# Deformable attention, local part: the interpolation factors and the query copies change engines, and the products of the factors change place

## The chip, the cores and the metric

The kernel runs on one core of a Trainium2 chip. A core has five engines that run side by side, each through its own queue in a fixed order: TensorE (PE in the profile; PEld is its weight load), VectorE (DVE), ScalarE (ACT), GpSimd (POOL), and SyncE (SP), which here only issues DMAs. They wait for one another through semaphores. The metric is the device time of one execution in microseconds; the median of three runs of the kernel before is 7593.62 us (7591.17 to 7601.04).

## The reference, cut to what matters

The model has four layers, each a mixer and a feed-forward part, on x of shape (4, 64, 64, 128). The change touches the mixer of layer 0 alone. Queries, keys and values are 1x1 convolutions followed by depthwise 3x3 ones. For each pixel, each of 4 heads of 32 channels looks at 9 points of the key and value images, placed on a 3x3 grid with step d = 1, 3, 5, 7 for the four heads and moved by a learned offset (dy, dx). A point between pixels is read bilinearly, and multiplied by a learned mask:

```
py, px = pixel + d * grid + offset            # per head, 9 points
sample = mask * sum over the 4 corners of (1 - |wy|) (1 - |wx|) image[corner]
logits = <query, sampled key> / sqrt(32);  p = softmax over the 9 points
out    = projection(sum over points of p * sampled value);  x = x + out
```

If no offset is over 1 in size, the corners of all 9 points lie in a small window round the pixel. The kernel finds the greatest offset, and runs a local program if it is at most 1, a general one with gathers if not. With these inputs the local one runs. In it, the weight of the neighbour at distance i = -1, 0, 1 from the grid point is a hat function: max(0, 1 - |offset - i|), for y and x apart, and the bilinear weight is the product of the two.

## The kernel before, in words

The stages run one after another. Function `deformable_near` is the local program; it occupies about 667 to 1723 us of the profiled span. It works on pairs of image rows, 128 pixels, one a partition: 128 steps T (4 images x 32 row pairs), in chunks c of four steps (c = T // 4), and 14 further steps (LAG) in which the second half of the work runs out.

Per step, the first half:
- `products` (L729) copies the queries of the row pair into qm, one of two tiles, spread so that eight columns of pixels at a time meet their own band of keys: two copies per step, on POOL (L737).
- `product` (L754): 64 matmuls on PE (L766) give S, the products of each pixel's query with a band of keys in three rows times four, for the four heads. S has one buffer a head, so the next step's product waits for its copy.
- `copy_products` (L772): four copies on ACT (L776) into band, double buffered by chunk.

Per chunk:
- `offsets` (L686) loads the offsets and masks of four steps (tile of) through SP.
- `hats` (L691) and `rows_of_hats` (L703) make the factors on POOL, L697 to L716: hat for x and y, three values each, and hy, the y factors times mask, widened to four rows, since the 128 pixels of a step are two rows and the lower one (a bit of the partition number, tile row) is shifted by one.
- `hat_products` (L718): four products on POOL (L724), one a head, make H[point, 4 rows, 3 columns], the weights of 12 neighbours. H is double buffered.
- `attention` (L778), on DVE: copies under a predicate (L785) shift each partition's band to its own columns; twelve products with H (L787) and a reduction (L794) give the logits lg, less their maximum (L804).
- `spread` (L807): the exponential on ACT (L810), the normalisation on DVE, then the weights p times H are written into dense rows A, nine products for heads 1 to 3 (L817); head 0, whose points overlap, through t0 (L823) and twelve copies and additions (L827 to L830).
- `write` (L832) sends A to DRAM, `read_dense` (L840) reads it back turned so that each step has its dense matrix D.

Per step, the second half, 14 steps later: `transpose` (L872, twelve on PE, three copies dt on ACT at L880), `weigh` (L884, 96 matmuls or fewer with the value blocks vb, L898), and once a chunk `values_done` (L905, copy oT), `projection` (L916, PE L919, ACT copy L921, two additions on POOL L922 and L923) and `store`.

The order is set by the loop at L947: `step(T, first, do, every)` calls a part at T = first, first + every and so on. `block` chains the PE blocks of a step, and `behind` and `tc.issue_after` tell the scheduler that a part isn't to be issued before a given instruction. Beyond that the scheduler of the language orders each engine's queue, so that the queues, and not the source alone, say what stands behind what. In ACT's queue of the steady part the exponential of chunk c - 1 stands between the band copies of the first and of the second step of chunk c.

Of the kernel before, what the change touches and what calls it, by code (L numbers as in the profile page):

```python
# [608 lines left out]
def deformable_near(k, dr, x, y, qd, kd, vd, od, masks, w_proj, b_proj):  # L609
# [25 lines left out]
    with ExitStack() as ctx:  # L635
# [14 lines left out]
        for t in qms:  # L650
            nc.gpsimd.memset(t, 0.0)
        row = wp.tile([128, 1], F32, tag="row", name="row")
        nc.vector.tensor_copy(row, bit[:, 0, 0, 3:4])

        As = []
        for i in range(2):
            As.append([wp.tile([128, 4, WB[g], 4, 3], F32, tag=f"A{i}{g}", name=f"A{i}{g}") for g in range(4)])
            for t in As[i]:
                nc.vector.memset(t, 0.0)

        dd = [[dr.tile([128, 4 * PP[g] + 12], F32, tag=f"dd{i}{g}", name=f"dd{i}{g}") for g in range(4)] for i in range(3)]
# [10 lines left out]

        Hs, bands, outs, vblocks, logits, ofs, hat_of, hy_of, queries = {}, {}, {}, {}, {}, {}, {}, {}, {}
        accs, lefts, inputs, project, stores = {}, {}, {}, [], []
# [15 lines left out]

        def hats(c):  # L691

            of = ofs[c]
            hat = hat_of[c] = sm.tile([128, 8, 3, 4, 3, 3], F32, tag="hat", name="hat", bufs=1)
            src = window(of, 0, [[81, 4], [9, 8], [3, 3], [1, 3]])
            part = lambda i: window(hat, i, [[9, 4], [108, 8], [36, 3], [3, 3]])
            nc.gpsimd.tensor_scalar(part(0), src, -1.0, 0.0, op0=ALU.mult, op1=ALU.max)  # L697
            nc.gpsimd.tensor_scalar(part(2), src, 0.0, None, op0=ALU.max)
            flat = hat.rearrange("p s a t n i -> p (s a t n) i")
            nc.gpsimd.tensor_tensor(flat[:, :, 1], flat[:, :, 0], flat[:, :, 2], op=ALU.add)  # L700
            nc.gpsimd.tensor_scalar(flat[:, :, 1], flat[:, :, 1], -1.0, 1.0, op0=ALU.mult, op1=ALU.add)

        def rows_of_hats(c):  # L703

            of, hat = ofs.pop(c), hat_of[c]
            mk = sm.tile([128, 2, 36], F32, tag="mk", name="mk")
            at = lambda i: window(mk, 36 * i, [[0, 4], [1, 36], [0, 3]])
            nc.gpsimd.tensor_copy(mk[:, 0].rearrange("p (a t n) -> p a t n", a=3, t=4), window(of, 72, [[3, 3], [81, 4], [1, 3]]))
            nc.gpsimd.tensor_scalar(mk[:, 1], mk[:, 0], row, None, op0=ALU.mult)
            nc.gpsimd.tensor_tensor(mk[:, 0], mk[:, 0], mk[:, 1], op=ALU.subtract)  # L710
            hy = hat[:, 0:4].rearrange("p s a t n i -> p s (a t n) i")
            h4 = hy_of[c] = sm.tile([128, 4, 36, 4], F32, tag="hy", name="hy", bufs=1)
            nc.gpsimd.tensor_tensor(h4[:, :, :, 0:3], hy, at(0), op=ALU.mult)
            nc.gpsimd.tensor_tensor(hy, hy, at(1), op=ALU.mult)
            nc.gpsimd.tensor_tensor(h4[:, :, :, 1:3], h4[:, :, :, 1:3], hy[:, :, :, 0:2], op=ALU.add)
            nc.gpsimd.tensor_copy(h4[:, :, :, 3], hy[:, :, :, 2])  # L716

        def hat_products(c, groups):  # L718

            if 0 in groups:  # L720
                Hs[c] = sm.tile([128, 4, 36, 12], F32, tag="H", name="H")
            H, hat, h4 = Hs[c], hat_of[c], hy_of[c]
            for g in groups:
                nc.gpsimd.tensor_tensor(  # L724
                    H[:, g].rearrange("p n (a c) -> p n a c", a=4), window(h4, 144 * g, [[4, 36], [1, 4], [0, 3]]),
                    window(hat, 108 * (4 + g), [[3, 36], [0, 4], [1, 3]]), op=ALU.mult,
                )

        def products(T):  # L729
            i = T % 32  # L730
            c, t = divmod(T, 4)
            if t == 0:
                bands[c] = [sm.tile([128, 3, 4, 4, CW[g]], F32, tag=f"band{g}", name=f"band{g}") for g in range(4)]
            qm = qms[T % 2]
            q = queries[T // 4]
            for h in range(2):
                after[0] = nc.gpsimd.tensor_copy(  # L737
                    window(qm, 256 * h, [[32, 2], [72, 4], [1, 8]]),
                    q[:, 2 * (i % 4) : 2 * (i % 4) + 2, 32 * h : 32 * h + 32].rearrange("p y (m x) -> p y m x", m=4),
                )  # L740
# [31 lines left out]
        def copy_products(T):  # L772
            c, t = divmod(T, 4)
            acc = accs.pop(T)
            for g in range(4):
                nc.scalar.copy(bands[c][g][:, :, t], acc[g].rearrange("p (a s) c -> p a s c", a=3))  # L776

# [29 lines left out]
        def spread(c):  # L807
# [13 lines left out]

            t0 = sm.tile([128, 36, 12], F32, tag="t0", name="t0", bufs=1)
            nc.vector.tensor_tensor(t0, H[:, 0], window(lg, 0, [[1, 36], [0, 12]]), op=ALU.mult)  # L823
            for ty in range(3):
                a0 = lambda m0, n: window(A[0], 12 * m0 + ty, [[60, 4], [12, n], [3, 4]])
                tap = lambda tx, s0, n: window(t0, 144 * ty + 12 * tx + s0, [[36, 4], [1, n], [3, 4]])
                nc.vector.tensor_copy(a0(0, 3), tap(0, 0, 3))  # L827
                nc.vector.tensor_copy(a0(3, 2), tap(2, 1, 2))
                nc.vector.tensor_tensor(a0(1, 3), a0(1, 3), tap(1, 0, 3), op=ALU.add)
                nc.vector.tensor_tensor(a0(2, 1), a0(2, 1), tap(2, 0, 1), op=ALU.add)  # L830

# [112 lines left out]
        products(0)  # L944
        hats(0)
        rows_of_hats(0)
        for T in range(128 + LAG):  # L947
            now[0] = T
            with behind():
                step(T, -1, products)  # L950
                step(T, -5, offsets, 4)
                with tc.issue_after(after[0].ins):
                    step(T, 0, lambda c: hat_products(c, (0, 1)), 4)
                    step(T, 1, lambda c: hat_products(c, (2, 3)), 4)
                    step(T, -2, hats, 4)
                    step(T, -1, rows_of_hats, 4)
                step(T, 4, attention, 4)
# [1664 lines left out]
```

## Time and profile before

| what | us |
|---|---|
| median of three runs | 7593.62 |
| profiled execution, time | 7610.45 |
| its span | 7608.4 |
| PE busy | 6501.1 (85%) |
| DVE busy | 4893.8 (64%) |
| ACT busy | 2698.1 (35%) |
| POOL busy | 1932.7 (25%) |
| granted PE clock, mean | 0.895 |

The busy shares are averages over stages with different limits; the stage of the change takes about a seventh of the span. In a row of groups stand the line, engine, operation, tiles, sizes (partitions x elements) and count, then busy time in us and mean ns of one, then the engine's idle time just before and what ended it. A row of the timeline has start and duration in us, engine, line, operation, and in brackets the idle time before it with its releaser; instructions that follow closely are merged (x6 is six).

### The profile page before, as it was taken

What the parts mean: (1) busy time and instruction counts of PE and PEld (TensorE: products, weight loads), DVE (VectorE), ACT (ScalarE), POOL (GpSimd) and SP (SyncE); (2) the same over time, 40 slices, a digit from 0 to 9 for tenths busy, and PEclk for the clock granted to TensorE, in tenths of its full rate; (3) what the DMA queues carried; (4) which work ended last, traced back from release to release, by engine and by line L of the source; (5) the groups of instructions that cost most, each with busy time, mean ns of one, the idle gap of its engine ahead of it and who ended that gap; (6) DMA issues with size and microseconds to landing.
All of it is one profiled execution on the core that took longest, in us unless ns stands there. A gap on an engine that the chain in (4) does not pass through costs nothing. (4 is left out here: it accounts for less than half of the span.)

```text
span 7608.4 us, 157410 instructions
## 1 busy us (share of the span) xinstructions
PE 6501.1 (85%) x63791; PEld 3520.3 (46%) x63791; DVE 4893.8 (64%) x11051; ACT 2698.1 (35%) x6141; POOL 1932.7 (25%) x1794
## 2 busy tenths in 40 slices
PE   7996777875788789899989999798897997998989
PEld 3343666662455543355555555445225234242244
DVE  2213888865377546678855656674884876857877
ACT  3331333333154325411155665565004022041056
POOL 0003666640011100055522222253012112120135
PEclk9997888897789899999988889797997997988989
DMA  4436677772400031310000000001101111111101
GB/s 119 102 84 196 197 233 233 232 223 80 147 1 2 19 68 23 96 39 24 18 15 9 9 10 5 9 1 35 39 20 53 25 40 34 26 33 40 24 23 31
DMA packets 673787, 498.13 MB, mean 65 GB/s; under 512 B 296822, under 2 KB 588600, under 8 KB 669208
## 3 DMA queue, kind: packets, MB, share of 16 engines
q1 hardware_dynamic: 510158, 399.80, 18.8%
q10 hardware_dynamic: 162890, 88.11, 4.4%
q8 instruction: 509, 8.34, 0.5%
q14 instruction: 230, 1.88, 0.1%
HBM read 335.28 MB, written 152.33 MB: 64 GB/s over the span
## 5 line engine op out<-in xcount | busy, mean ns | idle before, releaser
L2491 DVE TENSOR_TENSOR t<-S,q 128x1536 f32<-128x1536 f32 (+3 forms) x608 | 1156.9, 1948 | 122.7 <-PE S L2479 117.5
L2479 PE MATMUL S<-R,L 32*128 32x512 f32 x4096 | 734.8, 651 | 90.0 <-DMA R<-wd 78.5
L2507 PE MATMUL acc<-t,sum 128*32 128x512 f32 x4096 | 639.6, 608 | 0.0
L766 PE MATMUL S<-kpad,qm 32*64 32x288 f32 (+3 forms) x8192 | 379.4, 408 | 191.1 <-ACT band L776 125.5
L2193 PE MATMUL pe<-ew,yT 128*128 128x512 f32 x1024 | 482.2, 606 | 26.2 <-DVE xs L2199 23.1
L785 DVE COPY_PREDICATED band<-bit,band 128x384 f32<-128x384 int32 (+11 forms) x384 | 382.6, 1102 | 175.6 <-ACT band L776 141.7
L1792 PE MATMUL acc<-w,attT 128*64 128x264 f32 x4096 | 485.4, 390 | 10.5 <-DMA xtl<-xtd 10.5
L2479 PEld LDWEIGHTS S<-R,L 32*128 32x128 f32 x4096 | 200.5, 186 | 611.1 <-issue 280.0
L2513 ACT COPY agg<-acc 128x512 f32<-128x512 f32 x32 | 18.8, 586 | 1196.7 <-DMA L<-pd 609.0
L1785 POOL TENSOR_TENSOR w<-xtl,ei 128x528 f32<-128x528 f32 x256 | 332.3, 1320 | 307.6 <-ACT ei L1784 202.9
L2199 DVE SCALAR_TENSOR_TENSOR xs<-pe,gate,xs 128x128 f32<-128x128 f32 x1024 | 332.5, 345 | 97.5 <-PE pe L2193 80.8
L766 PEld LDWEIGHTS S<-kpad,qm 32*64 32x64 f32 x8192 | 278.6, 151 | 245.4 <-issue 141.7
L1788 DVE TENSOR_TENSOR w<-xtl,pe 128x1056 f32<-128x1056 f32 x256 | 320.3, 1251 | 99.2 <-ACT ei L1784 89.0
L1792 PEld LDWEIGHTS acc<-w,attT 128*64 128x64 f32 x4096 | 283.6, 137 | 196.7 <-DVE w L1789 38.6
L2202 ACT ACTIVATE sc<-pe,gate 128x128 f32<-128x128 f32 x1024 | 291.3, 374 | 201.4 <-PE pe L2193 193.3
L2522 POOL TENSOR_TENSOR o<-o,bf 128x512 f32<-128x512 f32 x32 | 40.7, 1271 | 1231.1 <-ACT o L2521 1231.1
L514 PE MATMUL dw<-pad,diag 32*32 32x512 f32 x6912 | 308.4, 613 | 12.2 <-issue 6.1
L2507 PEld LDWEIGHTS acc<-t,sum 128*32 128x32 f32 x4096 | 92.8, 108 | 458.6 <-issue 436.2
L2193 PEld LDWEIGHTS pe<-ew,yT 128*128 128x128 f32 x1024 | 186.2, 194 | 233.5 <-issue 151.1
L880 ACT COPY dt<-pt 128x512 f32<-128x512 f32 x384 | 204.5, 604 | 165.6 <-PE pt L878 165.2
L878 PE MATMUL pt<-ident,D 128*128 128x128 f32 x1536 | 231.6, 304 | 17.5 <-DMA D<-dd 9.2
L1680 PE MATMUL acc<-y,xsp 128*64 128x512 f32 (+1 forms) x1088 | 237.1, 597 | 1.9 <-DVE xsp L1655 1.9
(525 smaller groups left out, 13001.1 us busy)
## 6 DMA issues: line engine op xcount, KB each, us to landing
vb<-vd SPq DMA_DIRECT2D x272, 256.0 KB
D<-dd SPq DMA_DIRECT2D x128, 192.0 KB
D<-dd SPq DMA_DIRECT2D x128, 168.0 KB
D<-dd SPq DMA_DIRECT2D x128, 144.0 KB
w<-in_e_weight_dram ACTq DMA_DIRECT2D x16, 1024.0 KB
w<-in_e_weight_dram SPq DMA_DIRECT2D x16, 1024.0 KB
wd<-s SPq DMA_DIRECT2D x32, 512.0 KB
D<-dd SPq DMA_DIRECT2D x128, 120.0 KB
```

Of the source, the lines that this page charges most:

```text
L514: nc.tensor.matmul(acc[g][32 * c : 32 * c + 32], diag[r, j, tap, :], pads[j][r, y0 : y0 + 8, tx : tx + 64], start=(tap == 0), stop=(tap == 8),
L766: ins = nc.tensor.matmul(acc[g][64 * h : 64 * h + 64].rearrange("p (a s) c -> p a s c", a=3), qm[rows, h, m, :], keys, start=(m == 0), sto ...
L785: nc.vector.copy_predicated(flat[:, :, 0:n], bit[:, 0, :, i : i + 1].to_broadcast([128, 48, n]), flat[:, :, s : s + n])
L1785: nc.gpsimd.tensor_tensor(w2[:, 2:4], xt[:, 2:4, 0:2], window(ei, 0, [[0, 2], [0, 2], [1, 132]]), op=ALU.mult)
L1788: nc.vector.tensor_tensor(w1, xt[:, :, 1:3], window(pe, 0, [[0, 4], [0, 2], [1, 132]]), op=ALU.mult)
L1792: nc.tensor.matmul(acc[b // 2][64 * (b % 2) : 64 * (b % 2) + 64], attT[:, b // 2, hp, 64 * (b % 2) : 64 * (b % 2) + 64], src[:, b].rearran ...
L2193: nc.tensor.matmul(pe[h].rearrange("p e c -> p (e c)"), yT[:, 128 * t : 128 * t + 128], ew[:, 4 * h : 4 * h + 4, :].rearrange("p e c -> p ...
L2199: nc.vector.scalar_tensor_tensor(xt, pe[0][:, e, :], gate[:, t, e : e + 1], xt, op0=ALU.mult, op1=ALU.add)
L2202: nc.scalar.activation(sc[:, e, j, :], pe[1][:, e, :], AF.Copy, scale=gate[:, t, 4 + e : 5 + e])
L2479: nc.tensor.matmul(S[:, j, :], Ls[n % 2][r, ag, :], Rs[n % 2][r, ag].rearrange("p x y -> p (x y)"), start=True, stop=True)
L2491: nc.vector.tensor_tensor(t[:, j0:j1].rearrange("p u (x y) -> p u x y", x=8), S[:, j0:j1].rearrange("p u (x y) -> p u x y", x=8), qf[:, q0 ...
L2507: nc.tensor.matmul(acc[0][32 * h : 32 * h + 32, :], sum4, t[:, j, :], start=(u < 4), stop=(u >= 60))
```

## The change

Five things change, all in `deformable_near`:
1. The factors are made by ACT: for each distance i, Abs of (offset + a constant per partition, tile dist), then once Relu(1 - that). `hats_of_rows` makes the four row factors hy (four Abs, one Relu) at step 4c, `hats_of_columns` the three column factors (three Abs, one Relu) and a copy of the mask at step 4c + 1, both not before the last band copy of that step. The row bit now enters through dist, so the mask is applied once, by one POOL product (`masked`).
2. That product and the first two H products are called at step 4c + 2, the other two at 4c + 3, instead of at 4c and 4c + 1.
3. The query copies into qm go from POOL to ACT.
4. Head 0 is spread through a zeroed tile, shared, in which each point has its own slot: three products, and one reduction that adds up the slots of the same column, in place of t0 and twelve small operations.
5. The projection's result is written over oT instead of into a tile of its own.

The queues that the scheduler makes of it: PE's is the same as before, instruction for instruction. In the steady part POOL's has, per chunk, the masking product, four H products and the two additions of the projection. In ACT's, the first half of a query copy stands ahead of each step's band copies and the second half after them; the row factors stand between the band copies of the first step and the three dt copies ahead of the exponential; the column factors follow the band copies of the second step.

```diff
-        row = wp.tile([128, 1], F32, tag="row", name="row")
-        nc.vector.tensor_copy(row, bit[:, 0, 0, 3:4])
+        dist = wp.tile([128, 7], F32, tag="dist", name="dist")
+        for i in range(4):
+            nc.vector.tensor_copy(dist[:, i : i + 1], bit[:, 0, 0, 3:4])
+            nc.vector.tensor_scalar(dist[:, i : i + 1], dist[:, i : i + 1], 1.0 - i, None, op0=ALU.add)
+        for i in range(3):
+            nc.vector.memset(dist[:, 4 + i : 5 + i], 1.0 - i)
...
+        shared = wp.tile([128, 720], F32, tag="shared", name="shared")
+        nc.vector.memset(shared, 0.0)
...
-        def hats(c):
...
-        def rows_of_hats(c):
...
+        def hats(of, off, t, n, at):
+            for i in range(n):
+                nc.scalar.activation(
+                    window(t, i, [[3 * n, 4], [36 * n, 4], [12 * n, 3], [n, 3]]), window(of, off, [[81, 4], [9, 4], [3, 3], [1, 3]]),
+                    AF.Abs, bias=dist[:, at + i : at + i + 1],
+                )
+            return nc.scalar.activation(t, t, AF.Relu, bias=1.0, scale=-1.0)
+
+        def hats_of_rows(c):
+            hy = sm.tile([128, 4, 36, 4], F32, tag="hy", name="hy", bufs=1)
+            hats(ofs[c], 0, hy, 4, 0)
+            hat_of[c] = [hy]
+
+        def hats_of_columns(c):
+            of = ofs.pop(c)
+            hx = sm.tile([128, 4, 36, 3], F32, tag="hat", name="hat", bufs=1)
+            mk = sm.tile([128, 36], F32, tag="mk", name="mk")
+            with tc.issue_after(hats(of, 36, hx, 3, 4).ins):
+                nc.scalar.copy(mk.rearrange("p (a t n) -> p a t n", a=3, t=4), window(of, 72, [[3, 3], [81, 4], [1, 3]]))
+            hat_of[c] += [hx, mk]
+
+        def masked(c):
+            hx, mk = hat_of[c][1:]
+            nc.gpsimd.tensor_tensor(hx, hx, window(mk, 0, [[0, 4], [1, 36], [0, 3]]), op=ALU.mult)
...
-                after[0] = nc.gpsimd.tensor_copy(
+                nc.scalar.copy(
...
-                nc.scalar.copy(bands[c][g][:, :, t], acc[g].rearrange("p (a s) c -> p a s c", a=3))
+                after[0] = nc.scalar.copy(bands[c][g][:, :, t], acc[g].rearrange("p (a s) c -> p a s c", a=3))
...
-            t0 = sm.tile([128, 36, 12], F32, tag="t0", name="t0", bufs=1)
-            nc.vector.tensor_tensor(t0, H[:, 0], window(lg, 0, [[1, 36], [0, 12]]), op=ALU.mult)
-            for ty in range(3):
...
+            for tx in range(3):
+                nc.vector.tensor_tensor(
+                    window(shared, 13 * tx, [[60, 12], [3, 4], [12, 3]]), window(H, 12 * tx, [[36, 12], [3, 4], [1, 3]]),
+                    window(lg, tx, [[3, 12], [0, 4], [0, 3]]), op=ALU.mult,
+                )
+            nc.vector.tensor_reduce(
+                window(A[0], 0, [[1, 3], [60, 4], [3, 20]]), window(shared, 0, [[240, 3], [60, 4], [3, 20], [1, 3]]), axis=AX.X, op=ALU.add
+            )
...
-            o = sm.tile([128, 4, 128], F32, tag="o", name="o", bufs=1)
+            o = oT
...
-        hats(0)
-        rows_of_hats(0)
...
-                with tc.issue_after(after[0].ins):
-                    step(T, 0, lambda c: hat_products(c, (0, 1)), 4)
-                    step(T, 1, lambda c: hat_products(c, (2, 3)), 4)
-                    step(T, -2, hats, 4)
-                    step(T, -1, rows_of_hats, 4)
+                step(T, 2, masked, 4)
+                step(T, 2, lambda c: hat_products(c, (0, 1)), 4)
+                step(T, 3, lambda c: hat_products(c, (2, 3)), 4)
...
                 step(T, 0, copy_products)
+                with tc.issue_after(after[0].ins):
+                    step(T, 0, hats_of_rows, 4)
+                    step(T, 1, hats_of_columns, 4)
```

More of the change, by code (lines that the diff above doesn't have):

```diff
@@ L671, in deformable_near @@
                 eng.dma_start(dd[i][g][:, 4 * PP[g] : 4 * PP[g] + 12], zero[:, 0:12])
-        Hs, bands, outs, vblocks, logits, ofs, hat_of, hy_of, queries = {}, {}, {}, {}, {}, {}, {}, {}, {}
+        Hs, bands, outs, vblocks, logits, ofs, hat_of, queries = {}, {}, {}, {}, {}, {}, {}, {}
         accs, lefts, inputs, project, stores = {}, {}, {}, [], []
@@ L689, in offsets @@
             nc.sync.dma_start(ofs[c], od[b][:, 4 * c8 : 4 * c8 + 4, :])
-        def hats(c):
[L693 to L701, printed above, removed]
@@ L703, in rows_of_hats @@
-        def rows_of_hats(c):
[L705 to L716, printed above, removed]
+        def hats(of, off, t, n, at):
[5 more added lines that the diff above has]
+            return nc.scalar.activation(t, t, AF.Relu, bias=1.0, scale=-1.0)
@@ L721, in hat_products @@
                 Hs[c] = sm.tile([128, 4, 36, 12], F32, tag="H", name="H")
-            H, hat, h4 = Hs[c], hat_of[c], hy_of[c]
+            H = Hs[c]
+            hy, hx, _ = hat_of[c]
             for g in groups:
                 nc.gpsimd.tensor_tensor(
-                    H[:, g].rearrange("p n (a c) -> p n a c", a=4), window(h4, 144 * g, [[4, 36], [1, 4], [0, 3]]),
-                    window(hat, 108 * (4 + g), [[3, 36], [0, 4], [1, 3]]), op=ALU.mult,
+                    H[:, g].rearrange("p n (a c) -> p n a c", a=4), window(hy, 144 * g, [[4, 36], [1, 4], [0, 3]]),
+                    window(hx, 108 * g, [[3, 36], [0, 4], [1, 3]]), op=ALU.mult,
                 )
@@ L820, in spread @@
                     )
-            t0 = sm.tile([128, 36, 12], F32, tag="t0", name="t0", bufs=1)
-            nc.vector.tensor_tensor(t0, H[:, 0], window(lg, 0, [[1, 36], [0, 12]]), op=ALU.mult)
-            for ty in range(3):
[L825 to L830, printed above, removed]
+            for tx in range(3):
[6 more added lines that the diff above has]
+            )
         def write(c):
```

## The prediction, made before the changed kernel had run

> **What bounds the kernel now.** The stages run one after another: in the timeline no load of the next stage (L50) is issued before 1723.36 us, after the last store of this one. So what this stage gains, the end gains, though the chain of waits is followed back only to 5186 us and never reaches it. I began with the busy time by stretches, for the steady part of the stage, chunks 4 to 30:
>
> ```profile
> core 0: us, PE busy (x) PEld busy (x) DVE busy (x) ACT busy (x) POOL busy (x), PEclk, DMA share, GB/s
> 838.00:1636.00 798.00, 631.23 (x17880) 526.44 (x17880) 650.77 (x1379) 307.11 (x809) 520.72 (x646) 0.88 0.78 231
> ```
>
> DVE is busy 82%, PE 79%, DMA 78%: no engine is full, so something goes round in a ring. The waits (who waited for whom: total us, times, longest) for 860 to 1600 us, 24 chunks:
>
> ```profile
> POOL qm L737 <- PE S L766: 239.9, 65, 7.9
> ACT lg L810 <- DVE lg L804: 205.5, 24, 11.9
> ACT band L776 <- PE S L766: 128.0, 72, 4.8
> DVE band L785 <- ACT band L776: 117.6, 24, 7.6
> ...
> PE S L766 <- ACT band L776: 66.0, 16, 7.1
> ```
>
> 24 times DVE waits for ACT's band copies and 24 times ACT waits for DVE's logits: once per chunk each. The timeline of one chunk shows the ring:
>
> ```profile
> 1125.65 6.11 DVE L785 COPY_PREDICATED band<-bit,band 128x384 f32<-128x384 int32 x6 [5.03 <-ACT band L776]
> ...
> 1144.67 0.31 DVE L804 TENSOR_TENSOR lg<-lg,me 128x144 f32<-128x144 f32 x1
> ...
> 1145.01 0.32 ACT L810 ACTIVATE lg<-lg 128x144 f32<-128x144 f32 x1 [6.56 <-DVE lg L804]
> 1145.24 1.04 ACT L776 COPY band<-S 128x144 f32<-128x144 f32 x4
> ...
> 1145.64 4.48 PE L766 MATMUL S<-kpad,qm 32*64 32x144 f32 x64 [2.40 <-POOL hat L700]
> ...
> 1150.18 1.07 ACT L776 COPY band<-S 128x144 f32<-128x144 f32 x4 [1.95 <-PE S L766]
> ...
> 1151.08 0.18 DVE L830 TENSOR_TENSOR A<-A,t 128x16 f32<-128x16 f32 x1
> ...
> 1154.18 2.20 PE L766 MATMUL S<-kpad,qm 32*64 32x144 f32 x64
> ...
> 1156.43 1.07 ACT L776 COPY band<-S 128x144 f32<-128x144 f32 x4 [1.43 <-PE S L766]
> 1156.74 1.93 DVE L785 COPY_PREDICATED band<-bit,band 128x384 f32<-128x384 int32 x2 [5.48 <-ACT band L776]
> ```
>
> Attention (DVE) takes 1125.65 to 1144.98. The exponential behind it stands in ACT's queue ahead of the band copies of the chunk's second step, so it holds them, and with them the one set of S banks and PE. Then three band copies and two key products (4.48 us at the low clock, 2.20 at the full one) pass before the next attention at 1156.74. (The "POOL hat" behind 1145.64 is one of several semaphores; the copy at 1145.24 is what freed S.) Spreading ended at 1151.3 and DVE then idled 5.48 us. I call attention A and the rest B. Over chunks 4 to 28, read off the timeline in this way, A averages 19.04 us, B 11.58, the period 30.6; 30.68 from exponential to exponential.
>
> Why A is 19: POOL works beside it. DVE's groups by shape, 860 to 1600 us:
>
> ```profile
> L787 DVE TENSOR_TENSOR prod<-band,H 128x144 f32<-128x144 f32 x290 | 105.8, 435 | 0.0
> L785 DVE COPY_PREDICATED band<-bit,band 128x384 f32<-128x384 int32 x24 | 28.7, 1195 | 117.6 <-ACT band L776 117.6
> ```
>
> The same for the last chunk alone (1648 to 1667 us), where POOL has no factor left to make:
>
> ```profile
> L787 DVE TENSOR_TENSOR prod<-band,H 128x144 f32<-128x144 f32 x12 | 2.9, 330 | 0.0
> L785 DVE COPY_PREDICATED band<-bit,band 128x384 f32<-128x384 int32 x1 | 0.6, 605 | 7.0 <-ACT band L776 7.0
> ```
>
> In that chunk A is 15.10 us (1648.52 to 1663.61), with one POOL instruction of 0.79 us beside it.
>
> **What the Trainium skill says.** SBUF — State Buffer, Who interferes with whom: a DVE instruction with two SBUF inputs contends with a GpSimd instruction that reads SBUF, through a lock held for a whole instruction; ACT and PE wait on nobody. The rows above agree (435 against 330 ns, 1195 against 605). TensorE: Matmul & The Clock Gate, What's actually happening: an idle PE falls to half clock; agrees with 4.48 against 2.20 us for the same 64 matmuls. ScalarE: Activation LUTs, Table sets: abs and relu are in every set, so the new calls should load no table; no run here shows it.
>
> **The change, part by part.** Per chunk, POOL loses the factors (mean ns of L697 to L716: 1570+1247+763+611+257+428+269+982+981+880+498 = 8.5 us) and eight query copies (8 x 0.69 = 5.5), 14.0 of 21.3 us (busy 520.72 over 26, 20.0, as some overlap); it gains one masking product as L714 (0.98). What stays is 0.98 + four H products (1.17 each) + the two projection adds (2.6) = 8.3 us.
>
> Where that falls counts. In the changed order PE's sequence is the same instruction for instruction. POOL's is: mask product, four H products, two adds. The mask product waits for ACT's mask copy, which stands behind the exponential: one query half, the band copies, three Abs, oT, a Relu. That is 0.32+0.24+1.07+1.0+0.62+0.55+0.22 = 4.0 us after the exponential starts. H is then ready at 4.0+1.0+4.3 = 9.3 us and the adds end at 11.9, while the next attention starts near 11.5 and reads H 3.6 us later. So POOL moves out of A into B, where DVE only spreads (6.7 us) and idles. A goes from 19.04 to about 15.2.
>
> ACT gains per chunk seven Abs, two Relu, a mask copy and eight query halves. Their price: ScalarE: Activation LUTs, What ACT_TABLE_LOAD costs, gives 280 ns + 0.833 ns an element with a pointer bias, 186 without, 93 less back to back: Abs (144) 0.31, Relu (576, 432) 0.67 and 0.55, mask 0.22, query half 0.24 or less. The exponential of 144 without pointer should cost 306 and takes 323 in the trace. Sum 7x0.31+0.67+0.55+0.22+8x0.2 = 5.2 us, beside 11.8 us busy now (307.11 over 26 chunks): 17 us, under any period here. Bounds for one Abs: 0.23 (the exponential's 323 less 93) and 0.52, an estimate from VectorE's price for elements that stand apart (Vector Engine (DVE) Microarchitecture Reference, Measured stream behaviour on trn2: up to 2.5 against 1.05 ns a column). I take 0.31.
>
> On the ring: a query half (0.24) stands ahead of the band copies twice. Three Abs, Relu, mask and another half stand ahead of the three dt copies, which then end 5.9 us after the exponential instead of 3.5; PE wants them after its product and the projection, at about 5.4 us: 0.3 on average. The four row Abs and their Relu (1.9 us) fall under a PE stretch of 4.9 us before their dt copies are needed: nothing, or 1 us if Abs costs 0.52.
>
> DVE's spreading loses the product t0 and twelve small operations (2.4 us, 1148.86 to 1151.26) for three products (0.28 each, as the nine of L817 in 2.50 us) and a reduction over 720 (0.9, from L794's 1953 ns for 1728): 0.7 less, in the 5 us where DVE idles, so nothing; without that idle time it would be 0.7 a chunk. The lock with POOL may stretch spreading by at most POOL's 5.3 us, to 12. DMAs are the same; the load of the offsets (tile of) moves ahead of two value blocks in SP's queue and now waits for ACT's mask copy, which is done before the spreading that SP awaits just ahead of it. The constants cost under 1 us at the start, behind the wait for the zeroing DMAs (band at 695.29).
>
> **What is late next: PE.** With A at 15.2, ACT could release the key product at 15.2+0.65+0.24 = 16.1 us after attention's start. PE itself, in the 25 chunks from 5 to 29, ends what stands before that product at 12.7 to 19.5 us, mean 16.2. The later of the two, chunk by chunk, averages 16.9; now it starts at 19.7. It then starts with little idle time before it: in the seven chunks where PE idled under 2 us it took 3.8 instead of 4.26 on average; half of those stalls go too, I take 3.3. The rest: 4.0 (projection, weights, transposes, as now) + 0.3 (dt) + 2.33 (second product) + 0.31 + 0.24 (band, query half). Period 16.9+3.3+4.0+0.3+2.33+0.55 = 27.4, against 30.68.
>
> **The sum.** 26 periods from exponential 4 to 30: 26 x 3.3 = 86. The first four (27.4 us each now) lose part of A, but there the H products still fall into A: 2 to 2.5 each, with the first attention (21.3 us, waiting for H) about 12. The last one 2 (its A is 15.1 already). Together 100 us; tail after the last chunk unchanged. The profiled execution took 7610.45 us (span 7608.4), so 7510; taken off the median of the runs, 7593.6, 7494.
>
> **The rivals.** (1) Part of the gain stays out: PE's instruction fetch ("issue" before the key products and the value products, 22.4+37.3 us in 24 chunks) slows as DMA goes from 0.78 to 0.88 of its time, or Abs costs 0.52 and delays dt. PE ready at 17.7 on average and 0.6 more in B: period about 29.2, 26 x 1.5 + 9 = 48 saved: 7546. For it: DMA is the fullest resource after DVE. Against: 263 GB/s occurs in slices now.
> (2) More: the stalls before PE's 16.2 are themselves partly low clock. Period 26.2: 26 x 4.5 + 14 = 131: 7463. PE's busy 24.3 us a chunk is the floor.
> (3) Slower: POOL's five products (5.3 us) and spreading's two-input operations lock each other out in B, and H comes late. Attention reads H 15.1 us after the exponential against 9.3 when ready, so nothing happens until H is 5.8 late, and the gain of 3.3 is gone at 9.1. If each of spreading's 15 products waits for a whole POOL product, H ends near 19: period 31.7, 26 x 1 = 26 lost: 7620. Against: spreading has too few POOL instructions beside it to be held so often.
> (4) It does nothing: A stays at 19 because something else slows DVE. The last chunk speaks against it.
>
> **How the numbers follow.** A difference under 0.2% (15 us) is about what a measurement of this kernel cannot tell from none. Chances: computed case 0.59 (7475 to 7525), rival 1 0.21, rival 2 0.07, rival 3 0.09, rival 4 0.04. Faster 0.87, same 0.04, slower 0.09. The range, 7462 to 7562, leaves out rivals 3 and 4 and the ends of 1 and 2.
>
> **What would show it.** Right: attention near 15.2 us, products near 0.33 us, POOL under 9 us a chunk, period 27 to 28, PE's waits for ACT's band shrunk and "issue" first among PE's waits. Wrong: attention over 17 us; DVE waiting for POOL's H; Abs over 0.5 us; PE waiting for dt by more than 1 us a chunk; a table load beside Abs.

## The result, and the profile after

The changed kernel takes 7537.68 us (median of five runs, 7520.84 to 7547.03), the kernel before 7591.17 on the same chip (7572.84 to 7601.04): a ratio of 0.9931, 95% interval 0.9911 to 0.9951, or 53 us. The forecast was 7494, 44 us less than measured. The measured time lies outside the band of the computed case (7475 to 7525), inside the whole range (7462 to 7562), and close to the 7546 of rival 1.

The profiled executions, 7610.45 and 7520.84 us, are 89 us apart, more than the medians. The reason is outside the stage: the first load of the next stage (L50) is issued at 1723.36 us before and 1670.01 after, 53.3 us earlier, and the other 36 us arise in later stages whose code is the same. So the stage gains about what the medians differ by. Its 53.3 us split like this (A is attention, B what lies between one attention and the next, both over chunks 4 to 28; the exponentials are the ACT rows of L817, L810 before):

| us | before | after | forecast |
|---|---|---|---|
| A | 19.04 | 15.17 | 15.2 |
| B | 11.58 | 13.86 | 12.2 (27.4 less 15.2) |
| period, exponential 4 to 31 | 30.70 | 29.03 | 27.4 |
| gained up to exponential 4 | | 14.9 | 12 |
| gained in the 27 periods | | 45.2 | 88 |
| gained from the last exponential to L50 | | -6.8 | 0 |

Almost all of the shortfall is in B. The busy times by stretches for the steady part of after, 29 instead of 30.7 us a chunk:

```profile
core 0: us, PE busy (x) PEld busy (x) DVE busy (x) ACT busy (x) POOL busy (x), PEclk, DMA share, GB/s
830.00:1570.00 740.00, 615.42 (x17536) 502.05 (x17534) 581.08 (x1118) 416.32 (x1250) 187.18 (x179) 0.90 0.82 245
```

POOL's share is down from 65% to 25%, ACT's up from 38% to 56%. DMA is at 0.82, from 0.78, since the same bytes pass in less time.

The groups of DVE by shape in 24 chunks, 860 to 1560 us (busy time, mean ns of one, idle time before it):

```profile
L794 DVE TENSOR_TENSOR prod<-band,H 128x144 f32<-128x144 f32 x288 | 69.6, 327 | 0.0
L830 DVE TENSOR_TENSOR shared<-H,lg 128x144 f32<-128x144 f32 x72 | 68.2, 1057 | 0.0
...
L792 DVE COPY_PREDICATED band<-bit,band 128x384 f32<-128x384 int32 x24 | 15.6, 650 | 133.6 <-ACT band L783 133.6
```

The products of attention take 327 ns, as they did only in the last chunk before (330), and the first predicated copy 650 instead of 1195. Attention runs free of POOL. But L830, three products of spreading of the same size, take 1057 ns each. The timeline of an undisturbed chunk shows what they meet:

```profile
1052.03 0.32 ACT L817 ACTIVATE lg<-lg 128x144 f32<-128x144 f32 x1 [4.50 <-DVE lg L811]
...
1053.56 3.26 DVE L824 TENSOR_TENSOR A<-H,lg 128x144 f32<-128x144 f32 x9
...
1055.55 0.99 POOL L722 TENSOR_TENSOR hat<-hat,mk 128x432 f32<-128x432 f32 x1 [21.06 <-ACT mk L717]
...
1056.62 3.85 POOL L731 TENSOR_TENSOR H<-hy,hat 128x432 f32<-128x432 f32 x4
1056.66 3.12 DVE L830 TENSOR_TENSOR shared<-H,lg 128x144 f32<-128x144 f32 x3
```

Three DVE products in 3.12 us beside POOL products of 0.98 us: each DVE product lasts as long as one POOL product. The lock (DVE and POOL holding each other up while both work) has moved from attention to spreading, which ends 8.4 us after attention and not 6.7. H is ready at 1060.47, 8.4 us after the exponential.

Where B grew is in the waits, again 24 chunks, 860 to 1560 us (who waited for whom: total, times, longest):

```profile
DVE band L792 <- ACT band L783: 133.6, 24, 15.3
...
PE pt L884 <- DMA D<-dd: 38.4, 53, 3.1
PE out L904 <- issue: 36.0, 27, 3.3
...
PE S L773 <- issue: 15.4, 15, 2.4
...
PE out L904 <- DMA vb<-vd: 6.0, 9, 2.0
...
PE S L773 <- ACT band L783: 3.2, 4, 2.1
```

PE hardly waits for ACT's band copies any more (3.2 us, before 66.0): it no longer stands behind attention. In their place is a wait that the kernel before hardly had: for the loads of D, and some for the value blocks, 44.4 us or 1.85 a chunk. 24 chunks of before, 860 to 1600 us, show D alone:

```profile
PE pt L878 <- DMA D<-dd: 3.7, 2, 3.4
```

The waits for "issue" did not grow.

B is not the same in every chunk: in half of the 25 it is 10.5 to 13 us, in the other half 13 to 21. The timeline of chunk 11, one of the longest (B is 19.8):

```profile
1017.13 0.32 ACT L817 ACTIVATE lg<-lg 128x144 f32<-128x144 f32 x1 [2.34 <-DVE lg L811]
...
1020.16 0.48 PE L884 MATMUL pt<-ident,D 128*128 128x128 f32 x1 [0.68 <-DMA D<-dd]
...
1021.20 2.19 PE L884 MATMUL pt<-ident,D 128*128 128x128 f32 x9 [0.56 <-DMA D<-dd]
...
1023.18 0.54 SPq L759 DMA_DIRECT2D q<-qd  x1
...
1030.10 0.24 ACT L744 COPY qm<-q 128x64 f32<-128x64 f32 x1 [6.09 <-DMA q<-qd]
...
1036.85 3.53 DVE L792 COPY_PREDICATED band<-bit,band 128x384 f32<-128x384 int32 x6 [11.08 <-ACT band L783]
```

PE takes the D loads one at a time as they land. SP had sent these four only just before:

```profile
1013.79 2.63 SPq L850 DMA_DIRECT2D D<-dd  x4
```

This holds in general. For each step I took the time from the end of its last D issue to its first transpose: over 860 to 1560 us the median is 15.9 us in before and 7.3 in after, and at most 6.0 in the 22 steps where PE waits for D. The buffer of D is not what holds the load back: in after it had been free for 16.8 us (median) when the load was issued, in before for 9.8. D is late because it is issued late.

Then ACT waits 6.09 us for a query load that SP issued only at 1023.18, and the band copies stand behind that copy in ACT's queue. Chunks 19 and 27 show the same (6.6 and 6.9 us; the profile puts the first down to a transpose on PE, but it goes away in e5 with the late query load): every eighth chunk (an image has eight), where SP has 38 or 39 DMAs to issue instead of 32 on average. With the query copies on POOL, as before, such a wait would stand in POOL's queue and not ahead of the band copies; no run puts the copies back alone.

### The profile page after: what moved, and what is told of

The parts are those of the page before. It is cut to its first block, busy times and chain, and to the rows that moved or that the text cites. A ratio compares the mean times of both kernels' runs of the same rounds, so it can differ in the third digit from the quotient of the medians.

```text
span 7519.0 us, 156903 instructions
## 1 busy us (share of the span) xinstructions
PE 6475.0 (86%) x63791; PEld 3490.8 (46%) x63791; DVE 4812.9 (64%) x10774; ACT 2842.8 (38%) x6717; POOL 1518.8 (20%) x1218
## 3 DMA queue, kind: packets, MB, share of 16 engines
q14 instruction: 226, 1.85, 0.1%
## 5 line engine op out<-in xcount | busy, mean ns | idle before, releaser
L2518 ACT COPY agg<-acc 128x512 f32<-128x512 f32 x32 | 18.8, 586 | 1192.6 <-DMA L<-pd 855.4
L792 DVE COPY_PREDICATED band<-bit,band 128x384 f32<-128x384 int32 (+11 forms) x384 | 312.5, 929 | 186.4 <-ACT band L783 149.8
L773 PE MATMUL S<-kpad,qm 32*64 32x192 f32 (+3 forms) x8192 | 365.8, 405 | 72.4 <-ACT band L783 37.7
L884 PE MATMUL pt<-ident,D 128*128 128x128 f32 x1536 | 259.8, 319 | 66.3 <-DMA D<-dd 48.4
L884 PEld LDWEIGHTS pt<-ident,D 128*128 128x128 f32 x1536 | 214.6, 203 | 87.6 <-DMA D<-dd 52.3
```

What stands on the lines that cost most here:

```text
L773: ins = nc.tensor.matmul(acc[g][64 * h : 64 * h + 64].rearrange("p (a s) c -> p a s c", a=3), qm[rows, h, m, :], keys, start=(m == 0), sto ...
L792: nc.vector.copy_predicated(flat[:, :, 0:n], bit[:, 0, :, i : i + 1].to_broadcast([128, 48, n]), flat[:, :, s : s + n])
L884: ins = nc.tensor.transpose(pt[:, g, :], D[:, g, ty : ty + 382 : 3], k.ident)
```

## Experiments

The theory after the first look at the trace: attention is shortened by what was forecast, and the loss is in SP's queue, which issues some 33 DMAs a chunk and is occupied 86% of the time (77% before, summed from the durations and the short pauses of its instructions, 840 to 1540 us). The rivals: the DMA engines themselves (bytes), or ACT and PE.

**e1: is it the place of the H products?** Only that is put back.

```
-                step(T, 2, masked, 4)
-                step(T, 2, lambda c: hat_products(c, (0, 1)), 4)
-                step(T, 3, lambda c: hat_products(c, (2, 3)), 4)
+                step(T, 0, masked, 4)
+                step(T, 0, lambda c: hat_products(c, (0, 1)), 4)
+                step(T, 1, lambda c: hat_products(c, (2, 3)), 4)
...
-                    step(T, 0, hats_of_rows, 4)
-                    step(T, 1, hats_of_columns, 4)
+                    step(T, -2, hats_of_rows, 4)
+                    step(T, -1, hats_of_columns, 4)
```

> After, with the mask product and the four H products put back beside attention (their old steps 4c and 4c + 1), the factors two steps earlier; nothing left out. Theory (POOL and DVE hold each other up while both work): attention rises from 15.2 us by the 5 us of POOL work that comes back, by 1.3 to 2.6, to about 17; spreading, which loses it, falls from 8.4 to about 6.7 us. If the time between attentions is set by SP's queue, as I now think, the period stays near 29 and the time within 20 us of 7538; if attention still sets the period, it grows by 1.7 us x 27, to about 7585. Rival (the factors and query copies alone slowed attention, H products do not): attention stays at 15.2, spreading at 8.4.

Measured: 0.999 (0.9978 to 1.0002). All of the gain is gone, with the factors and query copies still on ACT. A is 18.79 us, B 11.99, spreading 5.8. The groups of e1, DVE by shape, 860 to 1600 us:

```profile
L794 DVE TENSOR_TENSOR prod<-band,H 128x144 f32<-128x144 f32 x289 | 141.5, 561 | 0.0
...
L830 DVE TENSOR_TENSOR shared<-H,lg 128x144 f32<-128x144 f32 x72 | 22.8, 438 | 0.0
```

and POOL:

```profile
L731 POOL TENSOR_TENSOR H<-hy,hat 128x432 f32<-128x432 f32 x97 | 101.9, 1079 | 2.0
```

The slow products have changed sides: attention's take 561 ns, spreading's 438. Five POOL products, 1.02 + 4 x 1.08 = 5.3 us, lengthen attention by 3.6: dearer than the 1.3 to 2.6 expected. B falls by 1.9 with it, and the period grows by 1.8 us, to 30.86; that is the 45 us. So the lock is shown, and that attention sets the period when it is long: with 18.8 us of it the rest of the change gains nothing that can be measured. With the longer period PE also waits for the band copies again and hardly for D (860 to 1560 us), and the D loads are issued 18.1 us ahead (median), not 7.3:

```profile
PE S L773 <- ACT band L783: 86.5, 23, 7.3
...
PE pt L884 <- DMA D<-dd: 3.9, 2, 2.3
```

So the new work on ACT doesn't make D late by itself; D is late when as many DMAs and bytes have to pass in a shorter period.

**e2: fewer bytes, as many DMAs.** The value tiles are zeroed once at the start (that edit isn't printed), so what isn't loaded is zero.

```
-                    t[:, q].rearrange("p s c -> p (s c)"),
-                    bass.AP(..., [[10752, 32], [128, 4], [1, 512]]),
+                    t[:, q].rearrange("p s c -> p (s c)")[:, 0:256],
+                    bass.AP(..., [[10752, 32], [128, 4], [1, 256]]),
```

> After, with each load of a value block cut to half of its columns (256 of 512 elements a partition), as many DMAs as before; the other half of the values is left at zero, so that much of the computation is left out. Theory (SP's issuing is what runs late: 33 DMAs a chunk, 24.5 us of a period of 29): hardly any change, period 28 to 29, 7520 to 7540. Rival (the DMA engines are full, 7.0 MB a chunk at 245 GB/s): 15% fewer bytes bring the stretch between attentions from 13.9 to about 10.7, the period to 26.2, the time to about 7463.

Measured: 0.9836 (0.9814 to 0.9858), 72 us less than after. A 15.20, B 12.09, period 27.26. The waits, 860 to 1560 us:

```profile
PE S L776 <- ACT band L786: 26.1, 14, 3.7
...
PE pt L887 <- DMA D<-dd: 9.0, 13, 1.1
```

PE waits for the band copies again, hardly for D. SP's queue is occupied for 90% of this shorter period, so the 86% of after was not a limit in itself. This spoke against the theory of SP's issuing alone.

**e3: as many bytes, more DMAs.**

```
-                nc.sync.dma_start(t[:, q]..., bass.AP(..., [[10752, 32], [128, 4], [1, 512]]))
+                for h in range(2):
+                    nc.sync.dma_start(t[64 * h : 64 * h + 64, q]..., bass.AP(..., [[10752, 16], [128, 4], [1, 512]]))
```

> After, with each load of a value block issued as two DMAs of 64 partitions, same bytes and same packets. Theory (SP's issuing): 8.5 more issues a chunk at 0.6 us are 5 us; SP's 24.5 us become 29.6, the period 31 to 33, the time 7590 to 7650. Rival (DMA engines full, or ACT's new work): no change, 7525 to 7550.

Measured: 1.0096 (1.0069 to 1.0123), 125 us more than after. A is 15.13 still, B 18.62, the period 34.1: 5.1 us longer, for 8.3 more issues a chunk of 0.6 us (0.59 the median of such an issue). The waits of 860 to 1560 us:

```profile
DVE band L792 <- ACT band L783: 220.7, 21, 26.1
...
PE pt L885 <- DMA D<-dd: 129.1, 113, 6.6
```

PE's wait for D is 129 us. This spoke for issuing and against bytes alone, with the DMA engines less busy than in after (0.73, 209 GB/s). Together: bytes and number of DMAs both matter, and D is where either shows.

**e4, e5: the query loads.** e4 issues them from ACT's queue; e5 leaves them with SP, in the same place of its queue, but a chunk ahead.

```
-            nc.sync.dma_start(queries[n], ...)
+            nc.scalar.dma_start(queries[n], ...)
```

> After, with the query loads issued from ACT's queue instead of SP's; nothing left out. Theory (SP's queue late): the three chunks in which ACT waited 6.1 to 6.9 us for a query load, with the band copies behind it, lose that wait, some 8 us each, and SP has one issue of 0.6 us less per chunk: 25 to 40 us faster than after, 7498 to 7513. Rival (the long stretches come from PE and ACT themselves, the query load happens to end beside them): ACT gains 0.6 us of issuing per chunk, 7538 to 7555.

Measured: 0.9974 (0.9962 to 0.9986): 33 us slower than after. A miss, whose reason stands in e4's timeline:

```profile
1143.05 2.99 SPq L841 DMA_DIRECT2D dd<-A  x4
...
1148.70 0.33 ACTq L759 DMA_DIRECT2D q<-qd  x1
...
1149.12 0.24 ACT L744 COPY qm<-q 128x64 f32<-128x64 f32 x1 [9.81 <-DMA dd<-A]
```

By the profile ACT stood there until a write of dd had landed, which has nothing to do with queries. In the trace the DMAs of this stage, of either queue, carry eight completion semaphores in turn, and the DMA that last used the semaphore of a query load is a write of dd in all 24 chunks from 860 us on. I read the wait as the load waiting for that semaphore to come free. With the band copies behind it, ACT lost 71.8 us in 13 such places between 860 and 1560 us. The Trainium skill (DMA: Bandwidth & Descriptors, Issuing engines are not separate DMA queues) says that DMAs from any queue run on the same engines, so that another queue saves the issuing time alone; here it brought less than that, a loss.

```
-            queries[n] = sm.tile([128, 8, 64], F32, tag="q", name="q")
+            queries[n] = sm.tile([128, 8, 64], F32, tag="q", name="q", bufs=3)
...
         rows_of_queries(0)
+        rows_of_queries(1)
...
-                if T % 4 == 1 and T < 124:
-                    rows_of_queries(T // 4 + 1)
+                if T % 4 == 1 and T < 120:
+                    rows_of_queries(T // 4 + 2)
```

> After, with a third query buffer, each query load one chunk earlier in the same place of SP's queue; as many DMAs, nothing left out. In e4 the load on ACT's queue stood waiting there for an unrelated write of dd that had been issued eight DMAs before it, with ACT's band copies behind it, so that run didn't test the query wait. Theory (late query loads cost the three long stretches of B, and hold nothing else): ACT's waits for q of 6.1 to 6.9 us vanish, three stretches are 5 to 8 us shorter: 15 to 24 us faster than after, ratio to before about 0.990 to 0.991. Rival (SP or the DMAs behind it are the bound on average, so that a stall taken away here comes back in the next chunk): within 8 us of after, 0.992 to 0.994.

Measured: 0.9928 (0.9901 to 0.9956): after's time. ACT waits for no query load any more, and B in chunks 11, 19 and 27 falls from 19.8, 21.0 and 19.6 to 15.8, 17.3 and 15.2. But in the chunks behind them it rises from 10.5, 11.2 and 11.0 to 13.6, 14.3 and 14.0: of 12.0 us, 9.2 come back at once. B averages 13.97 us against 13.86. The striking 6 us waits were a symptom.

**e6, e7, e9, e10: a wait in SP's queue.** In after SP waits for the store of x before it can issue the next load of xg, with D loads behind (before had this wait too, 35.3 us). SP's own waits, 860 to 1560 us:

```profile
SPq L876 <- DMA x<-xg: 45.2, 21, 2.8
```

e6 gives xg a third buffer, e7 also calls the query load two steps earlier.

```
-                inputs[0] = sm.tile([128, 4, 128], F32, tag="xg", name="xg")
+                inputs[0] = sm.tile([128, 4, 128], F32, tag="xg", name="xg", bufs=3)
```

> After, with a third buffer for xg, so that its load no longer stands in SP's queue waiting for the store ahead of it to land (46.8 us of SP's time in 24 chunks, 1.9 us a chunk), with D loads behind it. Nothing left out. Theory (SP's queue is late by as much as it is given: 5.0 us of issues more made the period 5.1 longer in e3): the period falls from 29.0 by 1 to 1.9 us, 27 to 50 us faster than after, ratio 0.987 to 0.990. Rival (bytes in flight are the bound, as half the value bytes gave 1.8 us a chunk in e2): SP runs ahead by 1.9 us and then waits for the DMAs that it awaits elsewhere; within 10 us of after, 0.992 to 0.995.

> After, with the third xg buffer and the query load called two steps earlier, which puts it ahead of four D loads in SP's queue, 2.6 us earlier. Nothing left out. Theory: the gain of e6, and 3 x 2.6 = 8 us of the query stalls: ratio 0.986 to 0.989. Rival: as in e6, 0.991 to 0.995.

Measured: 0.9927 (0.9903 to 0.9950) and 0.9928 (0.9903 to 0.9953), but they didn't test the wait for xg: the scheduler used the buffer to load a chunk earlier, in the same place of the queue, and SP waited there as long as in after (46.3 and 46.4 us). ACT's long waits for queries are gone in e7, and as in e5 the time doesn't move. e9 ties the load behind the D loads of its own step; e10 adds e5's queries.

```
-                nc.sync.dma_start(
+                lastD[0] = nc.sync.dma_start(
                     dense[t][...], ...)
...
-                nc.sync.dma_start(inputs[0], tokens(x, b, i - 1, 4))
+                with tc.issue_after(lastD[0].ins):
+                    nc.sync.dma_start(inputs[0], tokens(x, b, i - 1, 4))
```

> After, with the load of xg tied behind the D loads of its own step, so that in SP's queue it stands 16 or so DMAs behind the store that it waits for and not 5. The third buffer of e6 had not done that: the scheduler used it to load a chunk earlier, behind the same sort of store, and SP still waited 46 us there. Nothing left out, as many DMAs. Theory (SP's time is the bound, 1 us for 1 us, as in e3): SP has 1.9 us a chunk more, the period falls from 29.0 to between 27.1 and 28.1, 25 to 50 us faster than after, ratio 0.986 to 0.990. Rival (the bytes are the bound, as in e2): SP gains the time and loses it in longer issues and other waits, within 10 us of after, 0.992 to 0.995.

> After, with e9's place for the load of xg and e5's queries a chunk ahead. Nothing left out. Theory: e9's gain and, with SP no longer late, the 8 to 20 us of the query waits that e5 did not show: ratio 0.984 to 0.988. Rival: as in e9, 0.991 to 0.995.

Measured: 0.9939 (0.9919 to 0.9960) and 0.9948 (0.9929 to 0.9966), no better than after. e9's SP waits, 860 to 1560 us:

```profile
SPq L850 <- DMA D<-dd: 28.5, 60, 1.1
...
SPq L877 <- DMA D<-dd: 1.6, 1, 1.6
```

The 45 us at the load of xg are gone (1.6 left). In their place the D loads wait more for earlier DMAs (28.5 us, 12.2 in after), and issuing a write of dd takes 1.14 us on average instead of 0.83 (0.50 before). PE's wait for D stays at 41.3 us, since D is still issued only 8.1 us ahead (median). SP's time is therefore not simply the bound: the time that SP was given here came back as longer issues and waits for earlier transfers.

**e8: the old spreading of head 0.** The three products and the reduction are replaced by t0 and its twelve small operations, as in the diff of the change.

> After, with head 0 spread as before, through t0 and twelve small operations; nothing left out. The forecast put this part at nothing, being 0.7 us less in a stretch where DVE waits. Theory: spreading ends later than 8.4 us after attention, at 9 to 11 us, since the lock with POOL's products falls on more instructions; DVE still waits for the band after it, and the writes of A come later to SP by 1 to 2 us, of which SP hides most: within 15 us of after, ratio 0.992 to 0.995. Rival (the late writes reach the ring): period longer by the same 1 to 2 us, 27 to 50 us, ratio 0.997 to 1.0.

Measured: 0.9929 (0.9905 to 0.9954). Spreading ends 10.8 us after attention and not 8.4; the time doesn't move. The new spreading is worth nothing measurable here.

**e11: before, with only POOL's order turned round.**

```
-        hats(0)
-        rows_of_hats(0)
...
-                    step(T, 0, lambda c: hat_products(c, (0, 1)), 4)
-                    step(T, 1, lambda c: hat_products(c, (2, 3)), 4)
-                    step(T, -2, hats, 4)
-                    step(T, -1, rows_of_hats, 4)
+                    step(T, 2, lambda c: hat_products(c, (0, 1)), 4)
+                    step(T, 3, lambda c: hat_products(c, (2, 3)), 4)
+                    step(T, 0, hats, 4)
+                    step(T, 1, rows_of_hats, 4)
```

> Before, with only the order of POOL's work turned round: the H products at steps 4c + 2 and 4c + 3 (they were at 4c and 4c + 1), the factors at 4c and 4c + 1 (they were at 4c - 2 and 4c - 1). Nothing left out, factors and query copies stay on POOL. Theory (POOL work of any kind beside attention slows it, and POOL still has 20 us a chunk, most of a period): attention stays at 18 to 19.5 us, ratio 0.997 to 1.003. Rival (it is the products with two inputs, H's above all, that lock DVE out): attention falls to 16 or 17 us, ratio 0.993 to 0.996. If H comes late, DVE waits for POOL in attention and it is slower than before.

Measured: 1.0045 (1.0026 to 1.0064), slightly slower than before and outside both ranges. A is 19.07 us and attention's products take 436 ns, as before (435), but these are averages of two kinds of chunk. In 17 of the 25 chunks from 4 to 28 two of the four H products, late in POOL's queue behind the factors, still run beside the end of attention, and A averages 20.0 us. In the other 8 no H product runs beside it, only factors and query copies (14.8 us of POOL's time), and A averages 17.0: what the rival expected, and 1.8 over after's 15.2. So POOL's other work alone costs attention about 2 us in those chunks, and the H products could not be kept out of the rest. The new place of the H products gained nothing while all of POOL's work was left on POOL (e11), and taking that work away gained nothing without the new place (e1). What H products kept wholly out of attention would give by themselves is not shown. In the profiled execution the period is 31.04, 0.3 over before; why the runs are 0.45% slower is not settled.

**e12: the ring with fewer transfers.** One of the four loads of each value block; the rest of the value tiles is zero, as in e2.

```
-            for q in range(4):
+            for q in range(1):
```

> After, with one of the four loads of each value block only, at its full width: 6.4 DMAs and 1.7 of 7.1 MB a chunk fewer; the other three quarters of the values are left at zero, so that much of the computation is left out. It asks what the ring of attention, band copies and key products gives when no transfer holds it. Theory (the forecast's own working of the ring was right, and what was missing is the transfers): attention 15.2, the rest 12 us, a period near the forecast's 27.4, close to e2's 27.3; ratio 0.982 to 0.986. Rival (e2 was still held by its transfers, and the ring is shorter than the forecast worked out): as in the undisturbed chunks of after, 15.2 + 10.5 to 10.7, a period of 25.7 to 26.3, ratio 0.976 to 0.981. Seen apart by whether PE waits for ACT's band copies (the ring) or for D (transfers).

Measured: 0.9846 (0.9820 to 0.9872), as e2. A 15.38, B 11.46, period 26.88. The waits, 860 to 1560 us:

```profile
PE out L907 <- issue: 41.8, 35, 3.3
...
PE S L776 <- ACT band L786: 27.6, 16, 4.3
```

There is no wait for D left at all (D is issued 15.8 us ahead, median), and the period is only 0.4 below e2's, though it has half a megabyte and 6.4 issues a chunk fewer than e2. I take both to be at the ring's own length, 26.9 to 27.3. One more thing differs: the granted PE clock between 860 and 1560 us was 0.89 in after, 0.92 in e2, 0.94 in e12 and 0.82 in e3. The chunk's two late key products took no less time in e2 and e12 than in after (5.9 and 5.7 us together, against 5.6), so a faster clock isn't what shortened those; for PE's other work the runs don't part clock and transfers.

No kernel here that does all of the work beats the changed one: e5 to e8 have its time within their intervals, and e2 and e12 leave values out.

## Why the prediction was right in sign and 44 us short

- **What bounds the kernel, and A.** Right. The ring through attention set the period (e1: attention 3.6 us longer, the period back at 30.9). A was forecast at 15.2 and is 15.17. H was forecast ready at 9.3 us after the exponential and is at 8.4. POOL has 7.3 us a chunk (175.95 us in 700, 24.1 chunks), 8.3 forecast.
- **ACT's new work.** Right in sum, 4.5 us a chunk (16.2 against 11.75) for 5.2 forecast. The groups of after by shape, 860 to 1560 us:

```profile
L744 ACT COPY qm<-q 128x64 f32<-128x64 f32 x191 | 49.7, 260 | 132.9 <-PE S L773 113.4 <-DMA q<-qd 12.9 <-PE pt L884 6.6
...
L700 ACT ACTIVATE hy<-of,dist 128x144 f32<-128x144 f32 x96 | 36.0, 547 | 0.0
...
L704 ACT ACTIVATE hy<-hy 128x576 f32<-128x576 f32 x24 | 16.4, 685 | 0.0
```

  One Abs takes 547 ns from start to end, over the sign of 0.5 that was to show the forecast wrong; but they overlap, four of them in 1.48 us (at 1043.44 in the timeline of after), so that they start (1.48 - 0.55) / 3 = 0.31 us apart, the price used. Relu was forecast at 0.67 and takes 0.685. No table load stands between 730 and 1690 us.
- **Spreading.** Forecast 0.7 us shorter, with up to 5.3 more for the lock; it is 1.8 longer. Costing it at nothing was right: even 10.8 us (e8) leave the time as it is.
- **What is late next.** PE: right as far as it goes. With the value loads cut the period is 26.9 to 27.3 (e12, e2), for 27.4 forecast. Of the signs of being right, the period of 27 to 28 did not come, and D, not "issue", heads the list of PE's waits by row (38.4 us against 36.0).
- **The step that failed: "DMAs are the same".** Their number and bytes are, but they were costed at nothing, although the period in which they must pass went from 30.7 to 27.4. The working of PE's readiness (16.2 us on average) was taken from before, where D was there in time but for 3.7 us in 24 chunks; after, PE waits 44.4 us for D and value blocks, 1.85 us a chunk. The forecast's terms, measured in the same way over chunks 4 to 28, show where it falls:

| us | before | forecast | after | e2 | e12 |
|---|---|---|---|---|---|
| key product (the first of the last two) starts, after attention's start | 19.7 | 16.9 | 18.8 | 16.6 | 16.4 |
| it takes | 4.3 | 3.3 | 3.1 | 3.6 | 3.3 |
| to the second product | 4.0 | 4.3 | 4.3 | 4.2 | 4.1 |
| second product, to the next attention | 2.7 | 2.9 | 2.9 | 3.0 | 3.0 |

  Only the first term is off, by 1.9 us. The waits for D and value blocks that stand in it are 1.8 us a chunk in after, 0.1 in before, 0.4 in e2 and none in e12; with the value loads cut the term is near what was forecast. 29.03 - 27.4 = 1.6 us a chunk x 27 = 44 us of the sum. The tail, "unchanged" in the forecast, is 6.8 us longer, and the first chunks gained 3 more than the 12.
- **The rivals.** Rival 1 has nearly the number that came (7546, period 29.2), and it is the reason why the range held; but it came by another way: it let PE's waits for "issue" grow, which it took for instruction fetch (no run here shows what they are), or Abs be dear. The waits for "issue" before the key and value products went from 59.7 to 51.4 us in 24 chunks. What it had right is to doubt that the DMAs, busy 0.78 of their time, had room for a period of 27. The argument against it, that 263 GB/s occurs in slices, took a peak for a rate that holds: the 7.1 MB of a chunk would need 260 GB/s in 27.4 us (an estimate from after's 245 over 29.03 us), and no run here held more than 245. Rival 3's lock is there (L830, 1057 ns), but H was never late. Rival 4 is refuted by A, rival 2 by the period.

Open: why D is issued so late, that is, whether SP is held by its own issues, by the bytes on their way, or by the eight completion semaphores. e2 moves the bytes, e3 the issues, and each moves the period; e9 shows that they are not independent. Fewer but larger loads of the same bytes would help to tell them apart and were not tried.

## What to carry to other kernels

When a wait is taken out of a ring, work out again for the shorter period everything that has to pass once in it and was comfortable in the old one: the DMAs of a chunk at the rate that the stage really holds, and the queue that issues them. Where two engines lock each other out, what counts is which work they do side by side: here putting five small products back to their old moment cost the whole gain (e1), and the new moment alone brought none (e11). A long wait in one timeline (the 6 us for a query load) may only be the place where lateness shows; taking it away is the test.

## What the runs showed of the hardware beyond that

- A DVE product of 0.33 us beside a run of POOL products of 0.98 us took 1.06 us (the three of L830 in after), as if the two took turns. Not every pair does this: in before the first predicated copy of a chunk took 1.2 us on average, with the projection's addition (L923) beside it on POOL in 17 of 24 chunks, and in e11 it took 0.61 us in the 18 chunks with query copies and the first factor operation (L697) beside it, as with POOL idle (0.60 in after).
- Issuing a DMA from SP took 0.36 to 0.6 us as a rule (the medians of dd, D and value blocks in before are 0.36, 0.57 and 0.60), but single issues took up to 4.1 us in before and 3.8 in after. The mean for dd rose from 0.50 to 0.83 and, in e9, to 1.14, while those for D and value blocks stayed. That long issues tell of a full transfer path is my reading, and not shown.
- The load that waited for a store of 256 KB went out 5.6 to 7.1 us after the store's issue (after, 860 to 1560 us); ACT's copy ran 6.9 us after the issue of the query load of 256 KB that it waited for (chunks 11 and 27).
